# Where VectorE computes the four outer left sums of a two-layer graph network, and in what pieces they are stored

## The chip, the cores and the metric

The kernel runs on one core of one Trainium2 chip. The metric is the device time of one execution in microseconds (us). Lower is better.

## The reference, cut to what matters

There are 128 graphs, each of 128 nodes with 512 features. The first layer mixes neighbours with attention weights made from the adjacency matrix; the second multiplies every node's value vector by a softmax over the nodes. Both begin with a layer norm and a relu, and both add their result to their input.

```python
def reference(x, adj, nodemask, Wv, bv, aw, ab, Wk, bk, Wqk, Wv1):
    h = jnp.maximum(_layernorm(x), 0.0)
    Xw = h @ Wv + bv
    e = leaky_relu(sj[:, None, :] + si[:, :, None] + ab[0], 0.2)     # sj, si: columns of Xw @ aw
    t = adj * jnp.exp(e); t = t / (jnp.sum(t, axis=-1, keepdims=True) + 1e-12)
    H = 0
    for k in range(3):
        H = H + h @ Wk[k] + bk[k]
        h = jnp.einsum('bij,bjd->bid', t, h)
    x = x + jax.nn.relu(H)
    h = jnp.maximum(_layernorm(x), 0.0)
    q, k = jnp.split(h @ Wqk, 2, axis=-1)
    w = nodemask * jnp.einsum('bid,bid->bi', q, jnp.einsum('bij,bjd->bid', adj, k)) / sqrt(512)
    return x + jax.nn.softmax(w, axis=1)[:, :, None] * (h @ Wv1)
```

## The kernel before, in words

Everything is float32. The large products are done with seven half-size products in place of eight (the Strassen-Winograd scheme), so sums and differences of blocks of the left matrix ("left sums") and of the right matrix are needed beside the blocks themselves. Graphs are handled two at a time; two graphs are a pair, numbered p = 0 to 63 (`NP` = 64), and two pairs are a quad, numbered q = 0 to 31 (`NQ` = 32).

Layer 0 is the loop `for p in range(NP)`. In one pair TensorE does, in this order: the products of `y10` (seven products of 128x512, function `strassen`), the eight small matmuls of `inner` and `outer` that apply the attention matrix twice, and the seven products of `y2(p + 2)` (128x257) for the pair after next. TensorE's own order is written by hand: `ordered` (L91) chains its instructions. The other engines' orders come from a list scheduler that is steered by `behind(what, op)` (L86), which places an instruction right after another one of its engine. A line such as L86 or L91 in the profile is therefore that of the helper; the tile names tell which step it is. An engine executes its list strictly in order, so an instruction that waits holds up all that stand behind it on that engine.

In `strassen` ScalarE copies sums between the PSUM banks. The copy `s[:, 1] <- c` after the fifth product in the list (product 7, "the seventh product") is followed by VectorE's `ends[1, 1]`, which in `y10` is `end11`: bank `e` gets `s` added, then `t_from_blocks` transposes the attention matrix into `tt` (the first of the small matmuls reads it), then `end12` adds into bank `b`, and the scheduler is told to put `for_layer1(p - 1)` behind that.

`for_layer1` prepares layer 1. Layer 1 applies the seven-product scheme twice, once over the rows of nodes of a pair of pairs (the "outer" level) and once inside. The tile `fw` (128 partitions, 8 slots of 512 numbers each) holds the outer level's left matrices of one quad. Slots 0 and 2 are filled by four transposes of the quad's first pair, slots 4 and 5 by four transposes of its second pair (slot 4 is L21, a block that is needed for sums alone). Slots 1, 3, 6 and 7 are the four outer left sums. The transposes' input `hv` comes by a round trip through DRAM: `norm2` (ScalarE) writes `h`, SyncE stores it to `h2d`, and four DMAs load it back with another row order.

Where these stand in the kernel before:
- In an even pair (second pair of a quad): four transposes (L431), then the first two sums (L446, L447), then GpSimd's queue stores slots 0 to 3 (L439).
- In the odd pair after it: the other two sums (a `behind` L86 and L443), a store of slots 4 to 7, then the four transposes of the next quad.
- The last quad that layer 0 prepares (q = 30) gets its last two sums in pair 63.

After `for_layer1` VectorE has `outer`'s four additions that make `x1` (L625), the statistics of the second layer norm (L294), and the attention steps of the next pair. `y2` waits in turn for ScalarE's copies, which stand behind ScalarE's part of these steps.

The stores of `fw` go over GpSimd's DMA queue, which also carries `agb` (adjacency blocks, L111), the small round trip `pzd`/`pz` (L474, L476) and, in pairs 37 to 52, one load of prepared weights each (`rw<-rwd`). SyncE's queue carries the other transfers, in list order: `td` and `junk` (the attention matrix' round trip), `h2d`, `hv`, `atd` (the masked adjacency), `hd`, `ag`, `x1d`, `xg`. Layer 1 reads `fd` back in two halves (`load_left`). The last quad (q = 31) takes another way and isn't touched by the change.

Of the kernel before, what the change touches and what calls it, by code (L numbers as in the profile page):

```python
# [9 lines left out]
FP = mybir.dt.float32  # L10
# [6 lines left out]
def kernel(  # L17
# [25 lines left out]
    nc = tc.nc  # L43
    B, N, D = x.shape
    K = wk.shape[0]
    P = 128
    DC = D // P
    HC = DC // 2
    HD = D // 2
    G = 2  # L50
    S32 = 32
    Q = P // S32
    NP = B // G
# [5 lines left out]
    NQ = NP // 2  # L59
# [17 lines left out]
    done = {}  # L77
# [5 lines left out]
    def behind(what, op, *args, **how):  # L83

        with tc.issue_after(done[what]):
            return op(*args, **how)  # L86
# [109 lines left out]
    def combined(r, t):  # L196
        return dict(zip((5, 6, 7, 4, 1, 2, 3), t + [r[0, 0], r[1, 0], r[1, 1]]))
# [128 lines left out]
    HV, LEFT, Y2, PZ, T, TT, X1, HV2, FW = ({} for _ in range(9))  # L326
# [4 lines left out]
    FD = [dram.tile([P, 8, G, HC, N], FP, name=f"fd{q}", bufs=1) for q in range(NQ)]  # L331
# [3 lines left out]
    SLOT = {1: 0, 5: 1, 2: 2, 6: 3, 4: 5, 3: 6, 7: 7}  # L335
    L21 = 4
# [77 lines left out]
        transposed(HV.pop(p), hT)  # L414
        LEFT[p] = left_sums(hT)

    SUMS = {}

    def for_layer1(p):

        q, second = divmod(p, 2)
        if not second:
            if q:
                SUMS.pop(q - 1)()
            else:
                FW[0] = left.tile([P, 8, G, HC, N], FP, name="fw")
        f = FW[0]
        blocks, hv = f[:, L21:SLOT[4] + 1] if second else f[:, 0:SLOT[2] + 1:2], HV2.pop(p)
        for j in range(G):
            for k in range(2):  # L430
                done["c12"] = nc.vector.transpose(blocks[:, k, j].rearrange("p f (n b) -> p f n b", n=Q),  # L431
                                                  hv[:, j].rearrange("p n (k f a) -> p k f n a", k=2, f=HC)[:, k]).ins
        if second:
            fv = f.rearrange("p o j k n -> p o (j k n)")
            fd = FD[q].rearrange("p o j k n -> p o (j k n)")
            at = {o: fv[:, i] for o, i in SLOT.items()}
            def store_half(i):
                half = slice(4 * i, 4 * i + 4)
                nc.gpsimd.dma_start(fd[:, half].rearrange("p o n -> p (o n)"), fv[:, half].rearrange("p o n -> p (o n)"))  # L439

            def upper():
                behind("c12", nc.vector.tensor_sub, at[7], at[1], fv[:, L21])
                done["c12"] = nc.vector.tensor_sub(at[3], at[2], at[6]).ins  # L443
                store_half(1)

            nc.vector.tensor_add(at[5], fv[:, L21], at[4])  # L446
            done["c12"] = nc.vector.tensor_sub(at[6], at[5], at[1]).ins  # L447
            store_half(0)
            SUMS[q] = upper

    def y2(p, steps={}, gate=None, after="ln"):

# [27 lines left out]
    def spread_columns(p):  # L480
        for j in range(G):
            spread(PZ[p][:, j, :], Y2[p][:, j, 0, :1])
# [57 lines left out]
    def t_from_blocks(p):  # L540

        tt = TT[p] = front.tile([P, G, N], FP, name="tt", bufs=1)
        done["tt"] = behind("e", nc.vector.transpose, tt.rearrange("p g n -> p (g n)"),
                            TV.pop(p).rearrange("p g q i -> p (g q i)")).ins
# [34 lines left out]
    def own_set(p):  # L579
        return set2 if p == NP - 1 else set1  # L580
# [6 lines left out]
    def y10(p, steps):  # L587

        s = front.tile([P, 2, WP * 2], FP, name="s", bufs=1)[:, :, :D]

        def end12(b, t):
            done["c12"] = behind("tt" if 1 < p < NP - 1 else "rs" if p else "t", nc.vector.tensor_add, b, b, t).ins

        def end11(e, t):
            done["e"] = behind("rs" if p else "t", nc.vector.tensor_add, e, e, t).ins
            if p in TV:
                t_from_blocks(p)

        strassen(own_set(p), LEFT.pop(p), right10, s, False, {
            (0, 0): lambda a: None,  # L600
            (1, 1): end11,
            (0, 1): end12,
            (1, 0): lambda c: None}, steps, "warm" if p else "z",
            second="h2" if 1 < p < NP - 1 else "warm")
# [93 lines left out]
    def load_left(q, load, halves=(0, 1)):  # L698
        if q not in F:
            F[q] = f0 if q % 2 == 0 else back[2].tile([P, 8, G, HC, N], FP, name="f")  # L700
        for i in halves:
            half = slice(4 * i, 4 * i + 4)
            load(F[q][:, half].rearrange("p o j k n -> p (o j k n)"),
                 FD[q][:, half].rearrange("p o j k n -> p (o j k n)"))

# [51 lines left out]
    for p in range(NP):  # L757
        weights, weights_end = [], None
        if DC < p <= 2 * DC:
            weights = combine_steps(*OUTER)[p - DC - 1:p - DC]  # L760
            weights_end = lambda: rightl.update(combined(*OUTER))
        elif FIRST <= p < LAST:
            o, i = divmod(p - FIRST, 4)
            weights, weights_end = prepare(FACTORS[o], i, stage)

        def between():
            if p == 0:
                behind("t", norm0, 2)
                behind("rs", begin, 1)
                return  # L770
            if p + 2 < NP:
                behind("t", begin, p + 2)
            if p + 3 < NP:
                RS0[p + 3] = behind("left", statistics, xg[p + 3],
                                    middle=(lambda: [behind("aggr", step) for step in weights]) if weights else None, last="right")

        if p == NP - 1:
            behind("rs2", attention, p)
        def norms():
            if p and p + 3 < NP:  # L780
                behind("s7", norm0, p + 3, RS0.pop(p + 3))

        steps = {1: between, 3: norms}
        if p in T:
            steps[2] = lambda: t_transposed(p)
        if p > 1:
            steps[5] = lambda: masked(p, "ba")
        y10(p, steps)
        if p > 0:
            behind("c12", for_layer1 if p < NP - 1 else SUMS.pop(NQ - 2), *([p - 1] if p < NP - 1 else []))  # L790
        if p == NP - 2:
            f0 = w2[:, :8 * G * HC * N].rearrange("p (o j k n) -> p o j k n", o=8, j=G, k=HC)
            load_left(0, swdge)
        if p == NP - 1:
            for step in inner_sums(0, FACTORS[:4]):
                behind("c12", step)
        z = inner(p)
        if p == 0:
            y2(1, {2: lambda: RS0.update({3: behind("left", statistics, xg[3], "u2")})})
            behind("y10", behind, "hv", norm0, 3, RS0.pop(3))  # L800
            spread_columns(1)
            attention(1, lambda: begin(2))
        behind("c12" if p else "left", outer, p, z)
        if p + 4 < NP:
            load_x(p + 4)
        if 0 < p <= DC:
            behind("x1d", rows, rl[:, :, 1], wv1, (p - 1,))
        if p == 0:
            setup_ctx.close()
            left = layer0.enter_context(tc.tile_pool(name="left", bufs=1))  # L810
            stage_ctx = ExitStack()
            stage = stage_ctx.enter_context(tc.tile_pool(name="stage", bufs=2, side="right"))
        if p + 2 < NP:
            def ahead():
                attention_exp(p + 1, gate="aggr")
                attention_adj(p + 1)

            def statistics_and_ahead():
                norm2_statistics(p, middle=ahead)
                attention_t(p + 1, "rs2")  # L820
                t_by_blocks(p + 1)

            y2(p + 2, *(({2: statistics_and_ahead}, "t", "z") if p else ()))
        if weights:
            weights_end()
        if p + 2 < NP:
            behind("s7", seed_a)
            behind("s7", seed_e)
        elif p + 1 < NP:
            seeds_last()  # L830
        norm2(p)
        if p + 3 < NP:
            load_adj(p + 3)
        if p == LAST:
            stage_ctx.close()
            prep_ctx.close()
            early = ctx.enter_context(tc.tile_pool(name="early", bufs=1, side="right"))
            RW = {o: early.tile([P, 7, HD], FP, name=f"rw{o}") for o in FACTORS[:4]}
        if LAST <= p < LAST + len(PIECES):
            o, i = PIECES[p - LAST]  # L840
            behind("pzq", nc.gpsimd.dma_start, RW[o][:, i], RWD[o][:, i])
# [255 lines left out]
    sums = inner_sums(0, LATE)  # L1097
    for q in range(NQ - 1):
        if q:
            begin_quad(q)  # L1100
            catch_up(q)
            sums = inner_sums(q, LATE)
# [29 lines left out]
        sums = inner_sums(q + 1, EARLY)  # L1132
# [18 lines left out]
        if q == NQ - 2:  # L1151
            del hooks[5], hooks[6]
            sums = inner_sums(NQ - 1, LATE, back[2].tile([P, 8, G, HC, N], FP, name="f"))
# [13 lines left out]
    q = NQ - 1  # L1167
# [201 lines left out]
```

## Time and profile before

| what | value |
|---|---|
| median of 3 runs | 2217.33 us (2217.32 to 2218.16) |
| the profiled execution: its time | 2216.18 us |
| its span, first to last instruction | 2214.4 us |
| TensorE's mean granted clock | 0.999 |
| TensorE (PE) busy | 2201.6 us, 99% of the span |
| VectorE (DVE) busy | 1658.0 us, 75% |
| ScalarE (ACT) busy | 1235.9 us, 56% |
| GpSimd (POOL) busy | 733.2 us, 33% |
| DMA | 519.35 MB, mean 235 GB/s |
| start of layer 1's first product | 1417.28 us |

A line of the timeline has: start in us from the span's start, duration in us of the merged piece, engine, source line, operation, out<-in by the program's names, shapes, count; in brackets the idle time of the engine before it and what ended it. A line of the groups has the count, the busy time in us and the mean ns of one, and then the idle time before them with what ended it. DVE is VectorE, ACT is ScalarE, POOL is GpSimd, SP is SyncE, PE is TensorE. Matmuls are pipelined and their ends are modelled, so a short wait of TensorE need not show as idle time; the starts of its instructions show it.

### The profile page before, as it was taken

The numbers are of one execution on the slowest core, as the hardware profiler recorded it, in microseconds if no ns is written. First come the engines' busy times: TensorE is split into PE (matmuls) and PEld (weight loads), VectorE is DVE, ScalarE is ACT, GpSimd is POOL, SyncE is SP. The second block draws the span as 40 slices with busy tenths as digits, with TensorE's granted clock in tenths as the row PEclk, the third lists the DMA queues.
The fourth block names the chain that finished last, engine by engine and source line by source line (L and its number), as shares of the span: only waits on it lengthen the run. The fifth ranks groups of instructions, "written<-read, shape, count | busy, mean of one in ns | idle before, by whom it ended". The sixth has DMA issues, their size and how long they took to land.

```text
span 2214.4 us, 29461 instructions
## 1 busy us (share of the span) xinstructions
PE 2201.6 (99%) x8113; PEld 1535.6 (69%) x8113; DVE 1658.0 (75%) x4532; ACT 1235.9 (56%) x2857; POOL 733.2 (33%) x886
## 2 busy tenths in 40 slices
PE   9999999999999999999999999999999999999998
PEld 6666666666666666566666666688788878887886
DVE  6778777787878777777877777587677777776778
ACT  4555555555545555555555554456666666666665
POOL 2112122222222122221212121255655554555454
PEclk9999999999999999999999999999999999999999
DMA  7688788788878878888888786768887888888887
GB/s 210 198 239 245 219 249 247 238 251 236 251 226 254 243 242 240 236 249 231 249 241 237 230 234 199 275 195 237 229 254 228 235 241 240 229 234 235 238 232 181
DMA packets 424640, 519.35 MB, mean 235 GB/s; under 512 B 100839, under 2 KB 279015, under 8 KB 408603
## 3 DMA queue, kind: packets, MB, share of 16 engines
q1 hardware_dynamic: 379544, 382.27, 57.4%
q0 software_dynamic: 44640, 134.67, 22.9%
q8 instruction: 65, 1.06, 0.2%
q14 instruction: 101, 0.82, 0.1%
q10 hardware_dynamic: 290, 0.53, 0.1%
HBM read 295.26 MB, written 222.07 MB: 234 GB/s over the span
## 4 chain that ended last, share of the span: by engine, by line
PE 94%; DVE 2%; DMA 2%; SPq 1%; issue 0%; ACT 0%; DVEq 0%
PE a L91 28%; PE c L91 25%; PE b L91 25%; PE e L91 16%; DMA hv<-h2d 1%; SPq L538 0%; DMA td<-t 0%; DVE fw L431 0%; SPq L346 0%; DVE x L625 0%; DVE z L86 0%; DVE c L679 0%; DVE st L294 0%; PE a L284 0%; PE b L284 0%
## 5 line engine op out<-in xcount | busy, mean ns | idle before, releaser
L679 POOL TENSOR_TENSOR c<-s,c 128x512 f32<-128x512 f32 (+1 forms) x186 | 201.2, 1095 | 250.0 <-DVE s L679 244.9
L111 POOL DMA_DIRECT2D agb<-in_adj_dram x256 | 150.2, 593 | 328.2 <-DVE aT L86 231.6
L91 PE MATMUL a<-r,x 128*128 128x512 f32 x512 | 240.8, 592 | 0.0
L91 PE MATMUL b<-rw,in 128*128 128x256 f32 x884 | 212.0, 379 | 0.0
L439 POOL DMA_DIRECT2D fd<-fw x62 | 33.9, 547 | 461.1 <-DVE fw L447 262.7
L91 PEld LDWEIGHTS b<-rw,in 128*128 128x128 f32 x884 | 168.0, 190 | 23.3 <-issue 0.5
L91 PEld LDWEIGHTS a<-r,x 128*128 128x128 f32 x512 | 97.0, 190 | 95.7 <-issue 92.3
L86 DVE TENSOR_TENSOR e<-e,s 128x512 f32<-128x512 f32 x64 | 44.8, 699 | 158.5 <-ACT s L86 158.5
L86 ACT COPY s<-c 128x257 f32<-128x257 f32 (+1 forms) x128 | 61.6, 481 | 177.6 <-PE c L91 177.4
L86 ACT COPY b<-a 128x257 f32<-128x257 f32 (+1 forms) x128 | 59.3, 464 | 168.9 <-PE a L91 168.9
L679 POOL TENSOR_TENSOR c<-c 128x1024 f32<-128x1024 f32 x61 | 144.1, 2363 | 11.5 <-DVE c L679 11.1
L91 PE MATMUL a<-w,x 128*128 128x257 f32 x512 | 131.9, 380 | 0.1
L91 PE MATMUL b<-w,sx 128*128 128x257 f32 x512 | 132.0, 380 | 0.0
L431 DVE STREAM_TRANSPOSE fw<-hv 128x256 f32<-128x256 f32 x248 | 88.2, 413 | 48.9 <-DMA hv<-h2d 46.2
L91 PE MATMUL c<-t,sx 128*128 128x512 f32 x256 | 120.3, 592 | 0.0
L91 PE MATMUL b<-t,sx 128*128 128x512 f32 x256 | 120.3, 592 | 0.0
L91 PE MATMUL b<-r,sx 128*128 128x512 f32 x256 | 120.3, 592 | 0.0
L91 PE MATMUL c<-t,x 128*128 128x512 f32 x256 | 120.3, 592 | 0.0
L91 PE MATMUL e<-t,sx 128*128 128x512 f32 x256 | 120.3, 592 | 0.0
L679 DVE SCALAR_TENSOR_TENSOR junk<-agg,wscale,c 128x512 f32<-128x512 f32 x126 | 96.7, 767 | 29.8 <-POOL c L679 24.3
L679 ACT ACTIVATE c<-c,wcol 128x512 f32<-128x512 f32 x124 | 86.3, 719 | 55.9 <-DVE wcol L679 55.9
L91 PE MATMUL a<-rw,f 128*128 128x256 f32 x448 | 108.1, 379 | 0.0
(269 smaller groups left out, 5287.8 us busy)
## 6 DMA issues: line engine op xcount, KB each, us to landing
fd<-fw POOLq DMA_DIRECT2D x62, 1024.0 KB, 5.0
xg<-in_x_dram SPq DMA_DIRECT2D x64, 512.0 KB, 7.0
x1d<-x SPq DMA_DIRECT2D x64, 512.0 KB, 4.1
h2d<-h SPq DMA_DIRECT2D x64, 512.0 KB, 3.8
hd<-h SPq DMA_DIRECT2D x63, 512.0 KB, 3.0
hv<-hd SPq DMA_DIRECT2D x252, 128.0 KB, 3.4
hv<-h2d SPq DMA_DIRECT2D x248, 128.0 KB, 4.4
h<-h2d SPq DMA_DIRECT2D x62, 512.0 KB, 8.8
```

Source lines behind the costliest of these rows:

```text
L86: return op(*args, **how)
L91: done["mm"] = op(*args, **how).ins
L111: nc.gpsimd.dma_start(agb[p][c * S32:(c + 1) * S32].rearrange("p g q i -> p (g q) i"), v[c])
L431: done["c12"] = nc.vector.transpose(blocks[:, k, j].rearrange("p f (n b) -> p f n b", n=Q), hv[:, j].rearrange("p n (k f a) -> p k f n a", ...
L439: nc.gpsimd.dma_start(fd[:, half].rearrange("p o n -> p (o n)"), fv[:, half].rearrange("p o n -> p (o n)"))
L679: done[engine] = op(*args, **how).ins
```

## The change

The four sums of a quad are taken out of `for_layer1` and made into a function of their own, `outer_left_sums`. It is called from `end11` of `y10`, ahead of the addition into bank `e`, in every odd pair from 3 on: behind VectorE's last step of the layer norm (`rs`), and with the addition `e` behind the sums. The sums of quad q are thus made in pair 2q + 3. The store of `fw` is cut in four: slots 0 and 2 after the first pair's transposes, slot 5 after the second pair's; slots 1 and 3 of the quad before with the next quad's first pair, slots 6 and 7 of the quad before with its second pair. Slot 4 (L21) is stored no longer, and layer 1's second half load starts at slot 5. In pair 63 there is no `for_layer1`; the last quad's two remaining stores are issued from `end11`.

```diff
-    SUMS = {}
     def for_layer1(p):
         q, second = divmod(p, 2)
-        if not second:
-            if q:
-                SUMS.pop(q - 1)()
-            else:
-                FW[0] = left.tile([P, 8, G, HC, N], FP, name="fw")
+        if p == 0:
+            FW[0] = left.tile([P, 8, G, HC, N], FP, name="fw")
...
         if second:
-            at = {o: fv[:, i] for o, i in SLOT.items()}
-            def store_half(i):
-                half = slice(4 * i, 4 * i + 4)
-                nc.gpsimd.dma_start(fd[:, half].rearrange("p o n -> p (o n)"), fv[:, half].rearrange("p o n -> p (o n)"))
-            def upper():
-                behind("c12", nc.vector.tensor_sub, at[7], at[1], fv[:, L21])
-                done["c12"] = nc.vector.tensor_sub(at[3], at[2], at[6]).ins
-                store_half(1)
-            nc.vector.tensor_add(at[5], fv[:, L21], at[4])
-            done["c12"] = nc.vector.tensor_sub(at[6], at[5], at[1]).ins
-            store_half(0)
-            SUMS[q] = upper
+            store_left(q, slice(SLOT[4], SLOT[4] + 1))
+            behind("fd", store_left, q - 1, slice(SLOT[3], 8))
+        else:
+            store_left(q, slice(0, SLOT[2] + 1, 2))
+            behind("fd", store_left, q - 1, slice(SLOT[5], SLOT[6] + 1, 2))
+
+    def store_left(q, slots):
+        if q >= 0:
+            done["fd"] = nc.gpsimd.dma_start(FD[q].rearrange("p o j k n -> p o (j k n)")[:, slots],
+                                             FW[0].rearrange("p o j k n -> p o (j k n)")[:, slots]).ins
+
+    def outer_left_sums():
+        fv = FW[0].rearrange("p o j k n -> p o (j k n)")
+        at = {o: fv[:, i] for o, i in SLOT.items()}
+        nc.vector.tensor_add(at[5], fv[:, L21], at[4])
+        nc.vector.tensor_sub(at[6], at[5], at[1])
+        nc.vector.tensor_sub(at[7], at[1], fv[:, L21])
+        done["sums"] = nc.vector.tensor_sub(at[3], at[2], at[6]).ins
...
         def end11(e, t):
-            done["e"] = behind("rs" if p else "t", nc.vector.tensor_add, e, e, t).ins
+            sums = p > 2 and p % 2
+            if sums:
+                behind("rs", outer_left_sums)
+            done["e"] = behind("sums" if sums else "rs" if p else "t", nc.vector.tensor_add, e, e, t).ins
+            if p == NP - 1:
+                store_left(NQ - 2, slice(SLOT[5], SLOT[6] + 1, 2))
+                store_left(NQ - 2, slice(SLOT[3], 8))
             if p in TV:
                 t_from_blocks(p)
...
-            half = slice(4 * i, 4 * i + 4)
+            half = slice(SLOT[4] if i else 0, 8 if i else L21)
...
-        if p > 0:
-            behind("c12", for_layer1 if p < NP - 1 else SUMS.pop(NQ - 2), *([p - 1] if p < NP - 1 else []))
+        if 0 < p < NP - 1:
+            behind("c12", for_layer1, p - 1)
```

More of the change, by code (lines that the diff above doesn't have):

```diff
@@ L433, in for_layer1 @@
         if second:
-            fv = f.rearrange("p o j k n -> p o (j k n)")
-            fd = FD[q].rearrange("p o j k n -> p o (j k n)")
-            at = {o: fv[:, i] for o, i in SLOT.items()}
-            def store_half(i):
-                half = slice(4 * i, 4 * i + 4)
-                nc.gpsimd.dma_start(fd[:, half].rearrange("p o n -> p (o n)"), fv[:, half].rearrange("p o n -> p (o n)"))
-            def upper():
-                behind("c12", nc.vector.tensor_sub, at[7], at[1], fv[:, L21])
-                done["c12"] = nc.vector.tensor_sub(at[3], at[2], at[6]).ins
-                store_half(1)
-            nc.vector.tensor_add(at[5], fv[:, L21], at[4])
-            done["c12"] = nc.vector.tensor_sub(at[6], at[5], at[1]).ins
-            store_half(0)
-            SUMS[q] = upper
+            store_left(q, slice(SLOT[4], SLOT[4] + 1))
[14 more added lines that the diff above has]
+        done["sums"] = nc.vector.tensor_sub(at[3], at[2], at[6]).ins
     def y2(p, steps={}, gate=None, after="ln"):
```

## The prediction

> **What bounds the kernel now.** I read the page's busy times first, then the starts of TensorE's instructions pair by pair, then VectorE's timeline in pairs that run late and in pairs that don't, and last the turn from layer 0 to layer 1.
>
> ```profile
> PE 2201.6 (99%) x8113; PEld 1535.6 (69%) x8113; DVE 1658.0 (75%) x4532; ACT 1235.9 (56%) x2857; POOL 733.2 (33%) x886
> ```
>
> TensorE is busy for nearly the whole span, so a change on VectorE can gain only where TensorE waits. Since its ends are modelled, I take the starts of the first `e<-t,sx` of each pair:
>
> ```profile
> 89.35 1.88 PE L91 MATMUL e<-t,sx 128*128 128x512 f32 x4
> ...
> 864.72 1.88 PE L91 MATMUL e<-t,sx 128*128 128x512 f32 x4
> ...
> 1385.19 1.88 PE L91 MATMUL e<-t,sx 128*128 128x512 f32 x4
> ```
>
> These are pairs 2, 38 and 62. From 2 to 38 it is (864.72 - 89.35) / 36 = 21.538 us a pair, and no single pair of these is over 21.55: nothing on another engine costs time there. From 38 to 62 it is (1385.19 - 864.72) / 24 = 21.686, so 24 x 0.148 = 3.55 us are lost. The single starts put them in seven pairs: 38 (0.66), 40 (0.11), 42 (1.46), 45 (0.31), 46 (0.30), 48 (0.56), 52 (0.15), which adds to 3.55. Six are even: 3.24 us. All lie in the stretch with the extra `rw<-rwd` loads. In layer 1 the first aggregation matmul of each quad comes every 24.58 to 24.59 us without exception. So 3.55 us in layer 0, and 0.24 us at its end, is all that this change can reach.
>
> Pair 42 shows how an even pair gets late (VectorE, then TensorE):
>
> ```profile
> 960.43 0.70 DVE L86 TENSOR_TENSOR b<-b,s 128x512 f32<-128x512 f32 x1
> 964.35 1.42 DVE L431 STREAM_TRANSPOSE fw<-hv 128x256 f32<-128x256 f32 x4 [3.22 <-DMA hv<-h2d]
> 965.81 0.69 DVE L446 TENSOR_TENSOR fw<-fw 128x512 f32<-128x512 f32 x1
> 966.53 0.69 DVE L447 TENSOR_TENSOR fw<-fw 128x512 f32<-128x512 f32 x1
> 967.14 0.42 DVE L625 SCALAR_TENSOR_TENSOR x<-a,xg 128x256 f32<-128x256 f32 x1
> ```
> ```profile
> 971.95 1.13 PE L91 MATMUL c<-w,x 128*128 128x257 f32 x4 [1.19 <-ACT s L86]
> ```
>
> The `hv` loads land late, the transposes wait 3.22 us, and behind them in VectorE's list stand the two sums, then `x1`, the statistics and the attention step, on whose ScalarE part the seventh copy of `y2` waits; TensorE waits for that. The chain of waits goes the same way (DMA `hv`, four transposes, L446, L447, L625). Counted from the pair's `e<-t,sx`, pairs stall when `x1` starts after about 14.05 us (pair 50: 13.99, no stall; pair 40: 14.15, 0.11). In even pairs `x1` starts 2.80 us after the transposes, in odd ones 1.35. The difference, 1.45 us, is the two sums.
>
> [...] the sums took 682 to 692 ns here. [...] the 31 instances of each sum spread over 3 ns at most[...]
>
> **Part 1: the first two sums leave the even pairs' chain.** Each late even pair gains the smaller of its loss and 1.45 us: 0.66 + 0.11 + 1.45 + 0.30 + 0.56 + 0.15 = 3.23 us. The bounds: 0 if the loads land later by as much (below), 3.55 if pair 45 is mended too by its neighbours' earlier start. What is late next is TensorE itself.
>
> **Part 2: four sums in the odd pairs' wait.** The order of the built kernel puts them between `rs` and `e` in 29 of 31 quads. Pair 27:
>
> ```profile
> 633.14 0.16 DVE L308 SCALAR_TENSOR_TENSOR rs<-mv,rs 128x2 f32<-128x2 f32 x1
> 635.55 0.70 DVE L86 TENSOR_TENSOR e<-e,s 128x512 f32<-128x512 f32 x1 [2.25 <-ACT s L86]
> 636.16 0.43 DVE L86 STREAM_TRANSPOSE tt<-junk 128x256 f32<-128x256 f32 x1
> 636.59 0.70 DVE L86 TENSOR_TENSOR b<-b,s 128x512 f32<-128x512 f32 x1
> ```
> ```profile
> 638.11 0.59 PE L91 MATMUL a<-y,tt 128*128 128x256 f32 x2
> ```
>
> In the new build ScalarE's copy `c<-b` stands ahead of the two statistics steps in odd pairs as it already does in even ones, so `rs` ends where even pairs have it, 5.69 us after `e<-t,sx` (633.49 here). Three starts 0.60 apart and one of 0.73 (the last sum reads the one before; spacings of L86/L443 and L446/L447) put `e` 2.53 us after the first sum, at about 636.05: 0.5 us later than 635.55. So the wait is a little too short. Behind `e` stand `tt` and `b`. `tt` then ends at 637.10 and is wanted at 638.11, a margin of 1.0 us; `e` and `b` are wanted 0.43 and 0.86 later still and have 1.1. I take 0. Without that cover each 0.1 us beyond the margin would cost 30 x 0.1 = 3 us. The transposes of these pairs can start 0.7 us earlier than before where `hv` is there, since the 1.20 us of L86/L443 are gone; `x1` waits for TensorE at 12.66 anyway.
>
> **Part 3: pairs 61 and 63.** In 61 the sums fall between the steps that make the attention matrix, 1.8 to 2.4 us of delay for `td`; `junk` lands some 4 us before `e` is done and `tt` asks for it, so 0. In 63 the build puts one sum ahead of `z<-z`, two behind `aT`, one ahead of the reciprocal, all before `t`:
>
> ```profile
> 1407.02 0.29 DVE L86 SCALAR_TENSOR_TENSOR z<-z,ag 128x128 f32<-128x128 f32 x1 [0.72 <-ACT z L86]
> ...
> 1407.97 0.48 DVE L525 TENSOR_SCALAR t<-z,d 128x128 f32<-128x128 f32 x2
> ```
> ```profile
> 1408.31 0.53 PE L91 MATMUL a<-ident,t 128*128 128x128 f32 x2 [0.24 <-DVE t L525]
> ```
>
> TensorE already waits for `t`. Four sums of 0.60 are 2.40 us. Against them stand the 0.72 us that VectorE waits for ScalarE; 0.32 us, since pair 62 has no sums ahead of its `x1` and ScalarE's second statistics step comes that much earlier (its first now stands ahead of a copy that waits for TensorE); and two pauses of 0.1 us between dependent steps that a sum fills. 2.40 - 0.72 - 0.32 - 0.20 = 1.16: I take +1.1 us, bounds +0.7 and +1.9 (nothing earlier, and a wait for the store of slots 6 and 7).
>
> **Part 4: stores and loads.** Per quad four stores in place of two: 62 more issues of 547 ns on GpSimd's queue, 34 us in all. Behind the stores stand `agb`, `pzd` and `pz`; in pair 42 the queue sat idle 3.50 us between the store and `agb`, so 0.55 us more is covered; cost 0. One block of 256 KB less per quad in both directions is 62 x 0.262 = 16.3 MB of 519. In layer 1 nothing waits for loads; in layer 0 it can only help `hv`: 0 to 0.3 us, taken as 0. A slot's store is issued at least half a pair before the slot is written again, and landed in 7.9 us at most, so no new wait. On SyncE's queue `atd` moves ahead of `junk` and `hv` in odd pairs and `ag` behind `hd`; that is the even pairs' order already. Bounds: `junk` up to 0.6 us later or 1.6 earlier than odd pairs had it, `hv` likewise; with `x1` only 1.35 us behind the transposes, the latest landing that even pairs had (transposes at 12.70) would just pass. Taken as 0; at worst 1.5 us in the loaded stretch.
>
> **The sum.** -3.23 + 1.1 = -2.1 us: the profiled execution's 2216.18 becomes 2214.1 (floor: 2216.18 - 3.79 = 2212.4). The median of the runs is 1.15 us higher. TensorE's steady parts have no slack to vary, so I take half of that as more of the same lateness, which goes too: 2217.33 - 2.1 - 0.55 = 2214.7.
>
> **Rivals.**
> - *The lateness moves instead of going.* For it: the cause is the DMA, which stays; odd pairs get another queue order. Against: odd pairs with 1.35 us behind their transposes lost 0.31 us in all. Time: 2216.2 + 1.1 + up to 1 = 2217 to 2218.5, say 2217.8. Chance 0.17.
> - *More is gained.* The runs' extra 1.15 us is all lateness and goes, pair 63 costs little: about 2212.5. For it: the even pairs' rule is simple. Against: the 0.24 us at 1408. Chance 0.09.
> - *Slower: the four sums overrun the wait.* The place is `tt` in odd pairs, the price 30 times what exceeds the 1.0 us margin. It decides from 0.22 us of stall a pair (30 x 0.22 = 6.6, less 2.1 gained, is 4.5): the sums would have to take 1.0 us each. At 0.4 us a pair it is 2217.33 + 12 - 2.1 = 2227. Against: no sum took over 0.70 us. Chance 0.05.
> - *The change doesn't do what it says* holds for pairs 61 and 63 alone, as priced.
>
> **How the numbers follow.** The forecast has 0.69. What the measurement can tell from no change is about 0.2%, 4.43 us: faster is below 2212.9, slower above 2221.8. The forecast lies within; below 2212.9 I put most of the second rival, 0.08; above 2221.8 the slower rival, 0.05; within 0.87. The range takes in pair 63's bounds, the order of the queue and most of the first rival: 2212.7 to 2218.0.
>
> **What would show it.** Right: even pairs 38 to 52 at 21.54 us from `e<-t,sx` to `e<-t,sx`; L625 some 1.35 us behind the transposes in all pairs; in odd pairs four sums ahead of an `e` about 8.25 us into the pair with at most 0.1 us of idle time before it; a wait of 1.2 to 1.5 us of `a<-ident,t` in pair 63. Wrong: odd pairs over 21.54 (overrun), late pairs that stay, or no wait at `a<-ident,t`.

## The result and the profile after

The changed kernel takes 2215.53 us in the median of 22 runs (2213.39 to 2218.17); the kernel before, run beside it, 2218.40 us (22 runs, 2216.04 to 2222.02). The ratio is 0.9987, with a 95% interval of 0.9981 to 0.9993: 1.5 to 4.2 us faster. The profiled execution took 2213.94 us against 2216.18, its span 2212.2 us against 2214.4.

First the busy times, then the starts of the first `e<-t,sx` of pairs 2, 38, 44, 45 and 62 (timeline of TensorE, changed kernel):

```profile
PE 2200.0 (99%) x8113; PEld 1535.4 (69%) x8113; DVE 1700.5 (77%) x4532; ACT 1233.1 (56%) x2857; POOL 776.8 (35%) x948
```
```profile
88.79 1.88 PE L91 MATMUL e<-t,sx 128*128 128x512 f32 x4
...
864.15 1.88 PE L91 MATMUL e<-t,sx 128*128 128x512 f32 x4
...
993.38 1.88 PE L91 MATMUL e<-t,sx 128*128 128x512 f32 x4
...
1015.49 1.88 PE L91 MATMUL e<-t,sx 128*128 128x512 f32 x4
...
1381.63 1.88 PE L91 MATMUL e<-t,sx 128*128 128x512 f32 x4
```

Pairs 2 to 38 again take 21.538 us each. From 38 to 62 it is 517.48 us where 24 x 21.538 = 516.91: 0.57 us are lost, against 3.57 before. All of it is pair 44, which took 1015.49 - 993.38 = 22.11. So 3.00 us of losses are gone. The rest of the span: the start-up (pair 2 starts at 88.79, not 89.35) -0.56; pair 62, from its start to that of pair 63, 17.90 in place of 17.58, +0.32; from there to layer 1 15.78 in place of 14.52, +1.26; layer 1's 31 steps 751.77 us both times; the end -0.26. Together -3.00 - 0.56 + 0.32 + 1.26 - 0.26 = -2.24. The start-up varied from 88.8 to 90.5 between executions of all kernels here, so its part isn't the change's.

Pair 42, which stalled for 1.46 us before, with its transposes, `x1` and the seventh product of `y2` (VectorE, then TensorE, changed kernel):

```profile
962.39 1.43 DVE L426 STREAM_TRANSPOSE fw<-hv 128x256 f32<-128x256 f32 x4 [2.60 <-DMA hv<-h2d]
963.73 0.39 DVE L630 SCALAR_TENSOR_TENSOR x<-a,xg 128x256 f32<-128x256 f32 x1
```
```profile
969.26 1.03 PE L91 MATMUL c<-w,x 128*128 128x257 f32 x4
```

The loads are late here too: the pair starts at 950.30, so the transposes, which wait 2.60 us, start 12.08 us into it (12.70 before). But `x1` follows them by 1.34 us and not by 2.80, and TensorE's `c<-w,x` has no idle time before it.

Odd pair 27 (VectorE, the group of `e` over the whole kernel, ScalarE):

```profile
632.76 0.16 DVE L308 SCALAR_TENSOR_TENSOR rs<-mv,rs 128x2 f32<-128x2 f32 x1
632.84 0.68 DVE L445 TENSOR_TENSOR fw<-fw 128x512 f32<-128x512 f32 x1
633.44 0.68 DVE L447 TENSOR_TENSOR fw<-fw 128x512 f32<-128x512 f32 x1
634.04 0.68 DVE L446 TENSOR_TENSOR fw<-fw 128x512 f32<-128x512 f32 x1
634.76 0.69 DVE L448 TENSOR_TENSOR fw<-fw 128x512 f32<-128x512 f32 x1
635.37 0.69 DVE L86 TENSOR_TENSOR e<-e,s 128x512 f32<-128x512 f32 x1
635.97 0.43 DVE L86 STREAM_TRANSPOSE tt<-junk 128x256 f32<-128x256 f32 x1
```
```profile
L86 DVE TENSOR_TENSOR e<-e,s 128x512 f32<-128x512 f32 x64 | 44.5, 695 | 74.9 <-ACT s L86 74.9
```
```profile
630.92 0.57 ACT L86 COPY c<-b 128x512 f32<-128x512 f32 x1 [1.14 <-PE b L91]
631.40 0.30 ACT L86 ACTIVATE r<-mv,eps 128x2 f32<-128x2 f32 x1
```

The four sums stand where the order said. The pair starts at 627.24, so `e` comes at 8.13 us into it instead of 7.75, with no idle time before it; over the kernel the wait ahead of `e` fell from 158.5 to 74.9 us. No odd pair lost time. The last fence shows a by-product: ScalarE's copy `c<-b` now stands ahead of the statistics step in odd pairs.

Pair 63 (TensorE, then VectorE):

```profile
1406.26 0.61 PE L91 MATMUL a<-ident,t 128*128 128x128 f32 x2 [1.42 <-DVE t L524]
```
```profile
1402.02 0.69 DVE L445 TENSOR_TENSOR fw<-fw 128x512 f32<-128x512 f32 x1
...
1403.32 0.65 DVE L446 TENSOR_TENSOR fw<-fw 128x512 f32<-128x512 f32 x1
1403.89 0.68 DVE L447 TENSOR_TENSOR fw<-fw 128x512 f32<-128x512 f32 x1
...
1404.92 0.68 DVE L448 TENSOR_TENSOR fw<-fw 128x512 f32<-128x512 f32 x1
```

All four sums stand ahead of `t`, and TensorE waits for it 1.42 us where it waited 0.24.

### The profile page after: what moved, and what is told of

The parts are those of the page before. It is cut to its first block, busy times and chain, and to the rows that moved or that the text cites. A ratio compares the mean times of both kernels' runs of the same rounds, so it can differ in the third digit from the quotient of the medians.

```text
span 2212.2 us, 29502 instructions
## 1 busy us (share of the span) xinstructions
PE 2200.0 (99%) x8113; PEld 1535.4 (69%) x8113; DVE 1700.5 (77%) x4532; ACT 1233.1 (56%) x2857; POOL 776.8 (35%) x948
## 4 chain that ended last, share of the span: by engine, by line
PE 97%; DVE 1%; DMA 1%; ACT 0%; issue 0%; SPq 0%; DVEq 0%
PE a L91 28%; PE b L91 26%; PE c L91 26%; PE e L91 17%; DMA h2d<-h 0%; DVE c L684 0%; DMA junk<-td 0%; DMA hv<-h2d 0%; DMA td<-t 0%; PE a L284 0%; PE e L284 0%; PE c L284 0%; PE b L284 0%; DVE z L86 0%; PE e L221 0%
## 5 line engine op out<-in xcount | busy, mean ns | idle before, releaser
L438 POOL DMA_DIRECT2D fd<-fw x124 | 78.5, 636 | 498.9 <-DVE fw L426 471.7
L86 ACT COPY c<-b 128x257 f32<-128x257 f32 (+1 forms) x128 | 59.4, 464 | 98.5 <-PE b L91 98.4
```

Of the source, the lines that this page charges most:

```text
L438: done["fd"] = nc.gpsimd.dma_start(FD[q].rearrange("p o j k n -> p o (j k n)")[:, slots], FW[0].rearrange("p o j k n -> p o (j k n)")[:, s ...
```

## The experiments

Theory A: the gain comes from the two sums that leave the late even pairs' chain. Rival B: it comes from fewer bytes or another order of the queues, which make `hv` land sooner. Rival C: what pays is the use of the odd pair's wait itself. "Losses" below are what pairs 2 to 61 took beyond 21.54 us, in a kernel's trace. A "ratio" is to the kernel before, run beside the experiment, with its 95% interval; it is an estimate from all runs, and not exactly that of the two medians.

### One block less, and nothing else

The kernel before, with block L21 (slot 4) neither stored nor loaded; in both places:

```diff
-                half = slice(4 * i, 4 * i + 4)
+                half = slice(5 * i, 4 * i + 4)
```

> The kernel before with one thing of the change alone: slot 4 (L21) is neither stored nor loaded; the sums stay where they were. Theory A (the two sums leave the late even pairs' chain of waits): the losses of pairs 38 to 52 stay, 2 to 6 us over 21.538 a pair, the start of x1 in even pairs stays 2.80 us behind the transposes, time within 1 us of before. Theory B (fewer bytes make the hv loads land sooner): losses under 1 us, time some 2.5 us below before.

Measured: 2215.72 us (13 runs) beside 2218.14 for before (49 runs), ratio 0.9994 (0.9986 to 1.0002). Losses 4.45 us, in eleven pairs, the largest 40 (0.75) and 16 (0.90). The lateness stays as A says. The time speaks less clearly: the median is 2.42 us below that of before, which is what B expected and more than A's 1 us, but the interval holds 1.

> The kernel before with one block less stored and loaded, a second time, with more rounds. Theory A: losses in pairs 2 to 62 of 3 to 5 us in its trace, and a time within 0.1% of before. Rival B (fewer bytes alone bring a good part of the gain): losses under 1.5 us and a ratio of about 0.9987, as the changed kernel.

Measured: 2217.05 us (13 runs) beside 2218.05 (37), ratio 0.9992 (0.9984 to 1.0001); losses 2.32 us. The time is within 0.1%, as A had it, the losses below A's 3 and above B's 1.5. Each interval just holds 1, but both times the runs lie lower in the mean, by 1.9 and 1.6 us. So fewer bytes alone probably gain something in the kernel before; it isn't shown, and neither is that they gain nothing.

### The changed kernel with the block stored and loaded again

```diff
-            store_left(q, slice(SLOT[4], SLOT[4] + 1))
+            store_left(q, slice(L21, SLOT[4] + 1))
...
-            half = slice(SLOT[4] if i else 0, 8 if i else L21)
+            half = slice(4 * i, 4 * i + 4)
```

> The changed kernel, but slot 4 is stored with slot 5 and loaded again, so that it moves as many bytes as before. Theory A: as the changed kernel, 2.5 to 3 us below before, layer 0 losing under 1 us in pairs 38 to 52. Theory B: most of the gain is gone, losses of 2.5 us or more in pairs 38 to 52.

Measured: 2215.42 us (13 runs), ratio 0.9988 (0.9979 to 0.9996); no losses at all in pairs 2 to 61. The gain is there with the bytes of before, so the change doesn't need fewer bytes for it. B's first half is out as its cause, whatever fewer bytes would bring by themselves. B's second half, the order of the queues, has no run of its own; the starts of the transposes, under part 1 below, answer it for the even pairs.

### The four sums ahead of the next quad's transposes, not in the wait

All four sums of a quad stand ahead of the next quad's first transposes in the odd pair, behind `b`; in pair 63 they come behind `t`.

```diff
+        elif not second:
+            behind("c12", outer_left_sums)
...
-            if sums:
-                behind("rs", outer_left_sums)
...
```

> The changed kernel with the four sums in odd pairs behind the addition b and ahead of the four transposes, not in the wait for the seventh copy; in pair 63 they stand ahead of the inner sums, as the two did before. Theory A: even pairs are as in the changed kernel; odd pairs start their transposes at 11.9 us at the earliest and x1 at 13.3, below the 14.05 at which a pair stalls, so no loss there but where hv lands after 12.7; pair 63 waits 0.24 us for t, not 1.42. Time 3.5 to 4.5 us below before, 0.5 to 1.5 below the changed kernel. Theory C (it is the use of the wait that pays, VectorE's time being short): odd pairs lose 0.1 us or more each, time at or above before.

Measured: 2215.37 us (13 runs), ratio 0.9988 (0.9980 to 0.9996); losses 1.0 us; wait of `a<-ident,t` 0.06 us. The odd pairs have room for all four sums outside of the wait. C is out: the wait need not be used. The time is 2.8 us below before, not the 3.5 to 4.5 expected: what pair 63 saves doesn't show in it.

### Pair 63's sums behind `t`

```diff
-                behind("rs", outer_left_sums)
+                behind("t" if p == NP - 1 else "rs", outer_left_sums)
```

> The changed kernel with pair 63's four sums behind t instead of behind rs, in VectorE's 2.81 us wait for the copy of that pair. If pair 63's price is what the prediction says (four sums ahead of t), the wait of a<-ident,t falls from 1.42 us to 0.24 or less (pair 62's statistics now come earlier), and the time is 1.2 to 1.4 us below the changed kernel, about 4 below before. If the wait has another cause (a store that lands late, ScalarE's order), it stays over 1 us.

Measured: 2214.21 us (21 runs), ratio 0.9982 (0.9976 to 0.9989). The wait of `a<-ident,t` is gone, and from pair 63's start to layer 1 it takes 14.03 us (15.78 in the changed kernel). But pair 62 took 19.00 us in this trace; the last experiment takes that up.

### More sums in the wait

The changed kernel with two more sums behind the four (in the second kernel, `range(4)`, four more); they write slot 7 again with the same values.

```diff
+        for _ in range(2):
+            done["sums"] = behind("sums", nc.vector.tensor_sub, at[7], at[1], fv[:, L21]).ins
```

> The changed kernel with the sum L21 into slot 7 computed two further times (same values written again) behind the four sums, ahead of the addition into bank e, in every odd pair: six sums in the wait. The trace of the changed kernel has e at 8.14 us into the odd pair, and tt at 8.74 against a latest start of about 9.70, so the margin is about 0.95. Two more sums of 0.60 to 0.73 each put e at 9.3 to 9.6. If the price is the excess over this margin, as the prediction has it: 0.25 to 0.5 us of stall in each of 30 odd pairs, 7.5 to 15 us over the changed kernel. A theory in which the wait is not a limit at all (others absorb it): within 1 us. A theory in which there is no margin: 1.2 to 1.46 x 30 = 36 to 44 us.

Measured: 2228.41 us (3 runs), 12.9 over the changed kernel's median, though not run beside it; ratio to before 1.0039 (1.0023 to 1.0055). Each of the 29 odd pairs lost 0.35 to 0.36 us (pair 39: 0.48), and `e` came at 9.46: the limit of `e` is 9.10.

> As the kernel with two more sums, with four: eight sums in the wait. e is expected at 10.5 to 11.1 us into the odd pair. If every microsecond beyond the margin of 0.95 is paid in full: 1.45 to 1.97 us x 30 = 43 to 59 us over the changed kernel. The difference to the kernel with two more sums is then 30 x 1.2 to 1.46 = 36 to 44 us. If TensorE makes up part of it in the even pairs (a stall in the odd pair gives the even pair's loads time), less: 20 to 40.

Measured: 2266.63 us (2 runs), 51.1 over the changed kernel and 38.2 over the one with two more; ratio 1.0214 (1.0193 to 1.0234). Pair 27 of this kernel (VectorE; the line of 2.86 us is the four additional sums; then TensorE):

```profile
657.07 2.86 DVE L86 TENSOR_TENSOR fw<-fw 128x512 f32<-128x512 f32 x4
659.85 0.69 DVE L86 TENSOR_TENSOR e<-e,s 128x512 f32<-128x512 f32 x1
660.45 0.43 DVE L86 STREAM_TRANSPOSE tt<-junk 128x256 f32<-128x256 f32 x1
```
```profile
660.93 0.70 PE L91 MATMUL a<-y,tt 128*128 128x256 f32 x2 [1.54 <-DVE tt L86]
```

The pair starts at 648.93, so `tt` starts at 11.52 and the pair loses 1.81 us: the limit of `tt` is 9.71. In the changed kernel `tt` starts at 8.74, a margin of 0.96 us. Beyond it everything is paid, 29 times.

### All four sums in the even pair

The kernel before, with the other two sums moved to the even pair as well, behind the transposes: the change turned round.

```diff
-            SUMS[q] = upper
+            upper()
...
```

> The kernel before with all four sums of a quad behind the transposes of the even pair (the opposite of the change: two more sums ahead of x1). Theory A (sums between the transposes and x1 are paid one for one where hv is late): x1 then starts about 4.05 us after the transposes, the latest landing that costs nothing falls from 11.25 to about 10.0 us into the pair; with the landing times of the kernel before this is passed by 26 of 30 even pairs, and the excesses add up to 22.6 us against 3.2: 17 to 22 us slower than before. Theory C (what counts is only that the odd pair's wait was unused, not the even pair's chain): no more than 1 us from before.

Measured: 2294.69 us (4 runs) beside 2219.37, ratio 1.0347 (1.0321 to 1.0373): 75 us slower, not 17 to 22. The even pairs lost 24.3 us, in 26 pairs, about what was expected (22.6). The odd pairs lost 52.1, which nothing above had a term for. Pair 11 (it starts at 296.37; ScalarE, then TensorE):

```profile
301.14 0.30 ACT L86 ACTIVATE r<-mv,eps 128x2 f32<-128x2 f32 x1 [3.33 <-DVE mv L295]
301.47 0.20 ACT L300 ACTIVATE r<-r 128x2 f32<-128x2 f32 x1
301.58 0.57 ACT L86 COPY s<-e 128x512 f32<-128x512 f32 x1
302.04 0.59 ACT L86 COPY c<-b 128x512 f32<-128x512 f32 x1
```
```profile
302.69 1.98 PE L91 MATMUL c<-t,sx 128*128 128x512 f32 x4 [1.00 <-ACT c L86]
```

In odd pairs of the kernel before, ScalarE's copies stand behind the statistics step, which waits for VectorE's `mv` of the layer norm. If the even pair ran late on VectorE, `mv` is late, and TensorE waits for `c<-b`. This copy costs nothing up to 4.41 us into the pair (here 5.67, loss 1.26); before it usually starts at 3.7. Over all odd pairs what the copy was beyond 4.41 adds up to 44.8 of the 52.1 us. The changed kernel has the copy ahead of the statistics, so this second path is cut there.

### The loads of the prepared weights

The kernel before, with these loads in 8 pieces (pairs 37 to 44) in place of 16 (37 to 52):

```diff
-    PIECES = [(o, slice(i, min(i + 2, 7))) for o in FACTORS[:4] for i in range(0, 7, 2)]
+    PIECES = [(o, slice(i, min(i + 4, 7))) for o in FACTORS[:4] for i in range(0, 7, 4)]
```

> The kernel before with the prepared weights for layer 1 loaded in 8 pieces of up to four blocks (pairs 37 to 44) in place of 16 pieces of up to two (pairs 37 to 52). If these loads are what makes hv late: losses only in pairs 37 to 44 and none in 45 to 52; in pairs 37 to 44 more a pair than before (transfers of twice the size), total loss 2 to 8 us. If the lateness has nothing to do with these loads (a matter of place in the program or of chance): losses of some 3 to 4 us scattered through 38 to 52 and beyond, as before.

Measured: 2226.14 us (7 runs) beside 2219.37, ratio 1.0028 (1.0017 to 1.0039). Losses 10.4 us in pairs 38 to 45 and none in 46 to 61 (0.8 elsewhere). They went where the loads went, one pair beyond, and grew with the loads' size, to more than the 2 to 8 us expected. So most of the lateness comes with these loads.

### The kernel before, once more

> The kernel before, unchanged, for a second trace of it. Theory A says that the losses stand in even pairs of the stretch with the loads of prepared weights, again 3 to 5 us in sum, in much the same pairs; where the time of this execution is higher than in the first trace, the losses are higher by that much. If the losses of the first trace were a chance of that one execution, they are elsewhere or gone.

Measured: one execution, 2220.17 us. Losses 6.92 us: 5.55 in even pairs (38, 40, 42, 44, 46 with 0.75 to 1.15 each, 16 with 0.89, 52 with 0.21), the rest in odd ones. That is more than the 3 to 5 us expected, in much the same pairs. Against the first trace (2216.18) the time is 3.99 us higher, the losses 3.35. So the difference of these two executions is mostly lateness. Pairs 3, 27 and 29 (0.13, 0.11 and 0.34) are the second path: `c<-b`, behind a late `r<-mv`, starts at 4.55, 4.52 and 4.75 there, over the limit of 4.41 by just what each lost.

### A half load back behind `pzd`, beside the same kernel without that

In the changed order, GpSimd's queue issues layer 1's second half load ahead of the small store `pzd` in pair 62, at the time `td` is stored; before, it stood behind. This edit to the kernel with pair 63's sums behind `t` puts it back:

```diff
-            load_left(0, swdge)
+            load_left(0, swdge, (0,))
+            behind("pzd", load_left, 0, swdge, (1,))
```

> The kernel with pair 63's sums behind t, and in pair 62 the second half load of layer 1's first left matrices put behind the small store pzd on GpSimd's queue, as the kernel before had it (the changed kernel has it ahead of pzd, at the moment at which td is stored). In the traces the step from the issue of td to that of junk took 5.97 us before and 7.4 to 7.7 us with the changed order, and tt of pair 62 waited 0.93 us for junk before, 1.6 to 2.7 after. If the moved load is the cause: about 6 us again, tt's wait at most 1.0 us, pair 62 at 17.58 us (17.90 in the changed kernel, 19.00 in the kernel that this one edits), time 0.3 to 1.4 us below that kernel. If it is chance: 7 us or more again, and no difference.

> The kernel with pair 63's sums behind t, a second time and beside the one with the moved load. Time as in its first runs, 2214.2 us, 0.997 to 0.999 of before. In its trace: no wait of a<-ident,t, no loss in pairs 2 to 61 over 1 us, and, if the order of the loads in pair 62 matters, pair 62 at 17.9 us or more again.

Measured, on one chip: with the load behind `pzd` 2213.09 us (13 runs, ratio to before 0.9978, 0.9969 to 0.9986); without 2214.16 (17 runs, 0.9980, 0.9973 to 0.9987). The intervals overlap, so the traces have to tell. Pair 62's `td`, `junk` and `tt`, first with the load put back, then without (SyncE's queue, then VectorE):

```profile
1383.57 0.38 SPq L532 DMA_DIRECT2D td<-t  x1
...
1389.89 1.80 SPq L537 DMA_DIRECT2D junk<-td  x4
...
1394.80 0.45 DVE L86 STREAM_TRANSPOSE tt<-junk 128x256 f32<-128x256 f32 x1 [0.97 <-DMA junk<-td]
```
```profile
1381.38 0.38 SPq L532 DMA_DIRECT2D td<-t  x1
...
1388.92 1.81 SPq L537 DMA_DIRECT2D junk<-td  x4
...
1394.52 0.45 DVE L86 STREAM_TRANSPOSE tt<-junk 128x256 f32<-128x256 f32 x1 [2.87 <-DMA junk<-td]
```

From the issue of `td` to that of `junk` it took 6.32 us with the load put back, and 7.42 and 7.54 in the two traces without. The other traces agree: 7.4 to 7.7 us in all seven that have the load ahead of `pzd`, 6.0 to 6.4 in all seven that have it behind. So the delay of `junk` is the moved load's. What it costs varies: pair 62 took 17.58 us here against 19.00 and 19.19, which is 1.4 to 1.6 us, but the changed kernel's own trace lost 0.3 us and that of the kernel with the same bytes nothing. What else decides was not separated. `td` landed 1.2 us later where this load of 768 KB was issued 0.6 us behind it, and not 2.1 us behind it (7.5 against 6.3 us from its issue).

The losses of these two traces are 3.67 and 2.14 us, where the second was expected to show at most 1 us: of pairs 39 to 46 some lost time in both. With its profiled time of 2215.64 the first was far above its own median. The changed order isn't free of lateness; it has less of it.

## Why the prediction was right, step by step

**What bounds the kernel.** Right. One rule, a pair loses what `x1` is beyond 14.05 us or `tt` beyond 9.70, gives the loss of every pair within 0.08 us in eleven traces (before and after, all experiments but the ones with more sums and the one with all four in the even pair), with four odd pairs as exceptions, all in kernels with the old ScalarE order: pairs 3, 27 and 29 above and pair 3 in the first trace with a block less (`c<-b` at 4.76, loss 0.35), all four by the second path.

**Part 1, -3.23 us.** Right in size: losses fell by 3.00 us in the profiled pair of executions. Over several traces: before (twice) and the two with a block less 3.57, 6.92, 4.45, 2.32, mean 4.3; the changed kernel, that with the same bytes and the three with pair 63 mended 0.57, 0, 0, 3.67, 2.14, mean 1.3. The difference is again 3.0, though single traces overlap (2.32 and 3.67). The rival "the lateness moves" was true in part. In the same traces, pairs 38 to 52, the transposes of even pairs start at 12.04 us in the mean where they started at 11.59, those of odd pairs at 11.63 where it was 12.06; and `junk` in even pairs is issued at 2.56, not 1.95. So `x1` of even pairs gained 0.96 us in the mean, not 1.45. This also answers B's second half for the even pairs: with the new order their transposes start later, not sooner. With the starts of the transposes that the changed kernel had, two sums behind them would have cost its even pairs 6.2 us by the rule above (the transposes' start + 2.80 us, beyond 14.05), and those of the kernel with the same bytes 5.4; they lost 0.57 and nothing. Of the 3.0 us above, 2.4 are the even pairs'. The odd pairs lost 0.8 before and 0.2 after, and there B may be right in part: their transposes do start sooner, and the second path is gone. The store that `junk` of an even pair waits for, `td` of the odd pair before, landed in 2.7 to 3.5 us in the first trace of before and in 3.9 to 4.7 in that of the changed kernel (odd pairs 37 to 51, where the traces have it). Which step of the new queue order makes it slower was not separated. And "what is late next is TensorE itself" doesn't hold for pair 44, where `tt` waits for `junk`:

```profile
1001.06 0.70 DVE L86 TENSOR_TENSOR e<-e,s 128x512 f32<-128x512 f32 x1 [2.00 <-ACT s L86]
1003.64 0.45 DVE L86 STREAM_TRANSPOSE tt<-junk 128x256 f32<-128x256 f32 x1 [1.89 <-DMA junk<-td]
```

1003.64 - 993.38 = 10.26, which is 0.56 over the limit, and the pair lost 0.57.

**Part 2, cost 0.** Right: `e` at 8.13 where 8.25 was worked out, margin 0.96 where 1.0 was, no odd pair lost. The price of "30 times what exceeds the margin" held in both kernels with more sums (29 pairs show it). What the step left out is the other side of the ScalarE order that it noted: it takes the second wait path away. Before, that path cost 0 to 0.6 us in the traces here, so a small part of the gain over several runs may be due to that.

**Part 3, +1.1 us.** Right: the wait went from 0.24 to 1.42, +1.18. Pair 61 cost nothing.

**Part 4, cost 0.** Right for the 62 additional stores: no loss was traced to them, though they took 45 us more of the queue and not 34 (see the end). Right too, in the changed kernel, for the bytes, since with the bytes of before it took the same time. It failed in pair 62: the step looked at the queue in the steady pairs and priced the order there alone, not the two half loads at the turn to layer 1. It cost 0.32 us in the profiled execution, and 0 to 1.7 us in the six other traces with that order.

**The sum.** -2.1 forecast, -2.24 in the profiled pair. The agreement is partly luck: the terms named give -3.00 + 1.26 + 0.32 = -1.42, and start-up and end brought another 0.82. For the medians, the 1.15 us were too small an estimate of the lateness in the runs of before (their median was 2218.40, 2.2 over the profiled execution); the changed kernel's median is also 1.6 over its own. The half that was taken, 0.55, stands against 2.2 - 1.6 = 0.6.

**The slower rival** did not come: no sum took over 0.70 us, and it would have needed 1.0.

The lowest median of the study is that of the change with pair 63's sums behind `t` and the half load behind `pzd`: 2213.09 us, 0.9978 of before. The times don't separate it from the kernel without the moved load.

## What to carry to other kernels

Work that stood behind a late transfer and ahead of a step that others wait for was paid here in just those rounds in which the transfer was late (six even pairs of the first trace of before, 0.11 to 1.46 us each); moved to a place with measured margin it cost nothing here, and the margin (here 0.96 us, from the limit of `tt`) can be read off before anything is built. When a step is moved, look at the first and last rounds too, and at what each queue does there: sums ahead of `t` and a load that came too soon behind a small store gave back 1.26 and 0.32 us of the 3.00 that the steady rounds gained in the profiled execution, and the load cost up to 1.7 us in others. One profiled execution is one draw where transfers are late by chance: the same kernel's losses went from 3.57 to 6.92 us.

## What the runs showed of the hardware

- In the odd pairs of the changed kernel VectorE started a 512-wide addition 0.60 us after the one before, though each shows 0.68 us, and 0.72 us after one whose result it reads (L446 to L448).
- A store of `fw` of one slot or of adjacent slots took GpSimd 0.54 us to issue, before (544 ns in the median) as in the changed kernel (1.07 us for the two of an even pair); one of two slots that are not adjacent 0.73 us (1.45 for the two of an odd pair). All stores together took 78.5 us of the queue where they took 33.9 before: 45 us more, not the 34 that the prediction had.
- In pair 62 the 128 KB store `td` followed a load of 1024 KB by 0.3 us. From its issue to that of `junk`, which waits for it, it took 6.0 to 6.4 us in the seven traces where a second load was issued 2.1 us after it, and 7.4 to 7.7 us in the seven where that load was issued 0.6 us after it.
